# Products of zeros on TensorE ahead of the fold and behind the first image's last projection

## The chip, the cores and the metric

The kernel runs on one core of a Trainium2 chip. A core has a matrix engine (TensorE, PE in the profile, with its weight loads shown as PEld), a vector engine (VectorE, DVE), a scalar engine (ScalarE, ACT), a general engine (GpSimd, POOL), a queue engine (SyncE, SP), and 16 DMA engines. Each engine works through its own instructions in order and waits on semaphores for the others. The metric is the device time of one execution in microseconds (us).

## The reference

Eight images of 256 channels and 64 x 64 pixels pass through two layers, each with a residual:

```python
x = x + _L0_conv_ref(_gn(x), w_qkv, w_kg, b_kg, alpha, beta, w_proj)
x = x + _L1_conv_ref(_gn(x), w_off, b_off, w)
```

`_gn` normalises over 32 groups of 8 channels. The first layer projects to queries, keys and values; four heads of 64 channels attend to the 3 x 3 neighbourhood of each pixel:

```python
logits = jnp.einsum('bhdl,bhdkl->bhkl', q_flat, k_patch)
attn = jax.nn.softmax(logits, axis=2)
kernel = jnp.einsum('hkc,bhcl->bhkl', w_kg_g, cat) + b_kg.reshape(1, h, k2, 1)
out = alpha * conv_out + beta * attn_out
out = jnp.einsum('oc,bchw->bohw', w_proj, out)
```

Here `conv_out` and `attn_out` weight the 3 x 3 patches of the values by `kernel` and by `attn`. The second layer is a modulated deformable convolution: a 3 x 3 convolution gives 18 offsets and 9 masks for each pixel, four corners are gathered and blended at each of the nine positions, and a 256 x 256 product for each position sums them.

## The kernel before

Everything is fp32. On TensorE an fp32 product of 512 columns shows as two passes in the profile (two MATMUL records and two LDWEIGHTS records); a transpose shows as one. Channels lie on 128 partitions in two halves (`ct`), an image is cut into eight chunks of 8 rows (512 pixels).

The program is one stream per engine, written out by hand (`manual_schedule`): generators yield steps, and the main loop interleaves them. First `folded()` (line 225) multiplies `w_kgT` with `w_qkv` into `eff`, sixteen small products of nine columns, so that the generated kernel weights come straight from the normalised image. `first_stats` (L299) takes the statistics of image 0 on DVE while its chunks land, and `Norm` turns them into means and scales: `bn_aggr` (L192) into `mv`, a product with `gmat` (L197, `gn`), a few DVE steps on two columns, a second product (L208, `gv`), a square root on ACT and a reciprocal.

`attention(0)` then runs alone, without the second layer beside it, chunk by chunk. A chunk's work on TensorE, in the order of the profile: queries `psq` (L320, four passes for each half), keys `psk` (L351), logits `qk` (`products(0)`, L394), the generated weights `gen` (L437), `products(1)`, transposes `gt` (L456), and, between these, parts of the chunk before: `av` (L586), values `psv` (L351), `proj` (L602). It ends with `weights` (L529, transposes), `spread_weights` (L542) and `keys(0)` (L568, transposes). `masked` (L407, DVE) reads the logits of `products`, two tiles for each half of a chunk. `spread_weights` takes four PSUM tiles `wk`, one for each head, in a row; each head's product has nine rows of its own group of partitions, and DVE multiplies each tile by `near` (L550) into SBUF.

PSUM is shared out by pools: `ps_a` (four buffers of 512 columns, by far the most used), `ps_t` (two) and `ps_o` (two). A tile taken from a pool gets the buffer that was freed first, and its first writer waits for the last reader of the tile that had it before. In image 0, `proj` and `vk` use `ps_o` and `ps_t`; `eff`, `gn`, `gv`, `psq`, `psk`, `psv`, `qk`, `gen`, `gt`, `av`, `w` and `wk` all use `ps_a`, through `psum_a` (L182).

At the end of `attention(0)` the last `project` (L602), `add` (L613), `second_stats` (L617) and `Norm` follow each other, then `gn.means()` and `gn.ready()` as at the start. `prepare(0)` goes on from there: ACT scales the image into `z` (L773), TensorE transposes it (`ptab`, L791) for the table in DRAM from which the second layer gathers, and computes the offsets `om` (L838). From about 277 us the main loop runs the second layer of one image beside the attention of the next.

Of the kernel before, what the change touches and what calls it, by code (L numbers as in the profile page):

```python
# [9 lines left out]
F32 = mybir.dt.float32  # L10
# [7 lines left out]
P = 128  # L18
# [38 lines left out]
def preact_kernel(ctx: ExitStack, tc: tile.TileContext, a: dict, out: bass.AP):  # L57
# [17 lines left out]
    nc = tc.nc  # L75
# [3 lines left out]
    const = ctx.enter_context(tc.tile_pool(name="const", bufs=1))  # L79
# [81 lines left out]
    for i in range(min(2, B)):  # L161
# [7 lines left out]
        for o in range(H * WP, ENTRIES, P):  # L169
            n = min(P, ENTRIES - o)  # L170
# [10 lines left out]

    def psum_a(name):  # L182
        return ps_a.tile([P, 512], F32, tag="a", name=name)

    class Norm:

# [30 lines left out]
    def folded():  # L217

        ps = psum_a("eff")[:, : NT * HEADS * KK].rearrange(
            "p (c h k) -> p c h k", c=NT, h=HEADS  # L220
        )
        for ct in range(NT):
            for h in range(HEADS):
                for i in range(2):
                    nc.tensor.matmul(
                        ps[:, ct, h, :],
                        w_qkv[h // 2][:, 2 * (h % 2) + i, ct * P : (ct + 1) * P],
                        w_kgT[:, 2 * h + i, :],
                        start=(i == 0),
                        stop=(i == 1),  # L230
                    )
        return ps
# [62 lines left out]
    def first_stats(b, c):  # L295
        if c == 0:
            stats0[b] = p2.tile([P, NT, NC, 6], F32, tag="stats0", name=f"stats0_{b}")
        for ct in range(NT):
            nc.vector.bn_stats(  # L299
                stats0[b][:, ct, c, :],  # L300
                second[c][:, ct] if b == 1 else image[:, ct, c * N : (c + 1) * N],
            )
        if c == NC - 1:
            norm0[b] = Norm(stats0[b], f"0_{b}")
# [322 lines left out]
    def attention(b):  # L627

        xt = image
        first = b == 0  # L630
        jobs, due[:] = due[:], []
        gn = norm0[b]
        if b != 1:
            gn.means()
        stats = p2.tile([P, NT, NC, 6], F32, tag="stats", name=f"stats1_{b}")
        yield None
        gn = gn.gn if b == 1 else gn.ready()
        yield None
        xn = normed(xt, gn, 0, 2)
        for job in jobs[:1]:  # L640
            job()
        yield None
        d = added = None
        for c in range(NC):
            if c != 1:
                a_ = Attention(b, c, xn, stats)
                a_.q(0)
                if added:
                    added.second_stats()
                if c in (2, 5, 6, 7):  # L650
                    yield None
                a_.q(1)
                yield None if c == 4 else "quiet"
            else:
                a_ = follows
            ahead_of = c + 1 < NC
            at = 2 * (c % 2)
            a_.k(0)
            if ahead_of:
                xn = normed(xt, gn, c + 1, at, cts=(0,))  # L660
            yield None if ahead_of else "quiet"
            a_.k(1)
            if ahead_of:
                normed(xt, gn, c + 1, at, cts=(1,))
            if first:
                for n in (c - 1, c)[: 1 + (c == NC - 1)]:
                    if n >= 0:
                        first_stats(1, n)
            yield None if ahead_of else "quiet"
            if d and not first:  # L670
                d.keys(0)
            a_.products(0)
            for job in jobs[c - 1 : c] * (c in (2, 3)):
                job()
            yield None if c in (2, 3) else "quiet"
            a_.generated()
            a_.masked(0)
            yield None
            a_.products(1)
            a_.turned()  # L680
            yield "quiet"
            if d:
                d.weighted(0)
            else:
                a_.v(0)
            a_.masked(1)
            a_.summed()
            yield None
            a_.logits_1()
            a_.carry_k()  # L690
            if d:
                d.keys(1)
                d.carry_v()
                yield None
                a_.v(0)
                a_.logits_2()
                a_.softmax_1()
                yield None
                d.weighted(1)
                a_.twisted()  # L700
            else:
                a_.v(1)
                a_.logits_2()
                yield None
                a_.softmax_1()
                a_.twisted()
                follows = Attention(b, 1, xn, stats)
                follows.q(0)
            yield None
            if d:  # L710
                a_.v(1)
            else:
                follows.q(1)
            a_.softmax_2()
            a_.softmax_3()
            yield None
            if d:
                d.add(0, d.project(0))
                yield None
            a_.weights()  # L720
            if first and c == NC - 1:
                norm0[1].means()
            if d:
                d.add(1, d.project(1))
                added = d
            yield None
            a_.spread_weights()
            if first and c == NC - 1:
                norm0[1].ready()
            if first:  # L730
                a_.keys(0)
            yield None
            d = a_
        if not first:
            d.keys(0)
        added.second_stats()
        yield None
        d.weighted(0)
        yield "quiet"
        d.keys(1)  # L740
        yield "quiet"
        d.weighted(1)
        yield "quiet"
        if not first:
            later[0]()
        yield "quiet"
        d.add(0, d.project(0))
        d.add(1, d.project(1))
        d.second_stats()
        gn = Norm(stats, f"1_{b}")  # L750
        yield None
        if not first:
            later[1]()
        yield "quiet"
        gn.means()
        yield None
        gn.ready()
        yield gn.gn
# [424 lines left out]
    def finished(b, c, m):  # L1183
        if m == 0:
            state["y"] = p1.tile([P, NT, N], F32, tag="y", name=f"y_{b}_{c}")
        nc.scalar.copy(state["y"][:, m], state["po"][m])
# [14 lines left out]
        mybir.EngineType.Pool,  # L1201
    }
    with tc.manual_schedule(engines=ordered):
        ps = folded()
        for c in range(NC):
            first_stats(0, c)
        fold(ps)
        steps = fronts()
        for n in range(STEPS):
            next(steps, None)  # L1210

        for n in range(4):
            next(steps, None)
        for i in range(6):
            gather(i)
        next(steps, None)
        scale(0)
        scale(1)
        next(steps, None)
        sum_corners(0)  # L1220
        for i in range(6, LEAD, 2):
            next(steps, None)
            if holds:
                nc.gpsimd.memset(holds.pop(), 0.0)
            if i == 8 or i == 12:
                sum_corners(i // 2 - 2)
            gather(i)
            gather(i + 1)
            if i in (6, 10, 14):
                scale(i // 2 - 1)  # L1230
                scale(i // 2)
        next(steps, None)
        done = STEPS + STEPS_AHEAD
        last = None
        for n in range(B * SLOTS + 1):
            late, last = last, None
            if n > 0 and n % KK == 0:
                last = divmod(n // KK - 1, NC)
            for m in range(NT):
                if n < B * SLOTS:  # L1240
                    if m == 0:
                        transposes(*divmod(n, SLOTS))
                    if not last:
                        ahead(NB * n + 2 * m)
                if late and m == 0:
                    stored(*late)
                if n > 0:
                    product(*divmod(n - 1, SLOTS), m)
                if last:

                    finished(*last, m)
                    ahead(NB * n + 2 * m)
                    if n == B * SLOTS:
                        stored(*last, slice(m, m + 1))

                h = NT * n + m + 1
                goal = h * STEPS
                while (done - STEPS - STEPS_AHEAD) * STEPS < goal:
                    state["quiet"] = next(steps, True)
                    done += 1  # L1260
                if n < B * SLOTS:
                    gathers(NB * n + 2 * m)
# [76 lines left out]
```

## Time and profile before

| what | us |
|---|---|
| median of 3 runs | 4612.72 (4606.46 to 4614.89) |
| the profiled execution's own time | 4635.28 |
| its span, first to last instruction | 4633.3 |
| TensorE busy in the span | 4480.2 |
| first TensorE product (fold) | 16.73 |
| last projection of image 0 ends its issue | 224.5 |

The profile is of one execution. In the timeline each row gives the start, the time from the first start to the last end, the engine, the line, the operation with its tiles (written <- read), its size, the number of instructions, and in brackets how long the engine was idle before it and what ended that. A row of waits gives the total in us, how often, and the longest. The granted clock of TensorE is 1.00 or 0.50 in this profile, and it changes in steps of 3.41 us.

### The profile page before, as it was taken

How to read it: one execution, taken by the hardware profiler on the slowest of the kernel's cores; microseconds unless marked ns; L12 is line 12 of the kernel's file. 1: busy time of each engine (PE TensorE's matmuls, PEld its weight loads, DVE VectorE, ACT ScalarE, POOL GpSimd, SP SyncE). 2: the span in 40 equal slices, each digit the busy share in tenths (PEclk: the TensorE clock that was granted, in tenths of full speed). 3: DMA queues.
4: the chain of work that ended last, by engine and by line, in shares of the span. 5: the costliest groups of instructions: out<-in, count | busy, mean ns of one | idle time of the engine just before them, and what ended most of it. 6: DMA issues, size and time to landing. Idle time of an engine off the chain costs nothing.

```text
span 4633.3 us, 77608 instructions
## 1 busy us (share of the span) xinstructions
PE 4480.2 (97%) x25344; PEld 2332.3 (50%) x25344; DVE 4130.8 (89%) x10183; ACT 2514.2 (54%) x5280; POOL 2783.1 (60%) x2850
## 2 busy tenths in 40 slices
PE   8989999999999999999999999999999999998888
PEld 4445554555545555455554555555554555543344
DVE  6669999999999999999989999999999999988777
ACT  3345556555565555555555555655556555554444
POOL 0046655666555665566655665556655666568887
PEclk9999999999999999999999999999999999999999
DMA  4078889888998899988899888998899888899998
GB/s 143 28 230 294 304 312 368 314 301 303 310 385 297 294 312 320 369 295 306 301 338 331 298 307 311 354 331 297 299 315 373 296 287 302 296 335 333 352 336 317
DMA packets 445761, 1412.46 MB, mean 305 GB/s; under 512 B 46430, under 2 KB 63070, under 8 KB 445228
## 3 DMA queue, kind: packets, MB, share of 16 engines
q0 software_dynamic: 331776, 1208.11, 74.4%
q1 hardware_dynamic: 111836, 196.82, 11.8%
q8 instruction: 199, 3.26, 0.3%
q10 hardware_dynamic: 1744, 2.59, 0.2%
q14 instruction: 206, 1.69, 0.1%
HBM read 1275.97 MB, written 131.36 MB: 304 GB/s over the span
## 4 chain that ended last, share of the span: by engine, by line
PE 86%; DVE 4%; DMA 4%; issue 2%; POOL 2%; ACT 1%; another core or an unknown queue 0%; POOLq 0%; DVEq 0%; ACTq 0%; SPq 0%
PE po L1171 38%; PE pt L1146 10%; PE psk L351 5%; PE psq L320 5%; PE proj L602 5%; PE psv L351 5%; PE om L838 5%; PE av L586 3%; DVE s L1116 3%; PE vk L568 2%; PE qk L394 2%; DMA g<-table,idx 2%; PE wk L542 2%; PE gen L437 1%; DMA x<-in_x_dram 1%
## 5 line engine op out<-in xcount | busy, mean ns | idle before, releaser
L1092 POOL DMA_INDIRECT g<-table,idx x2304 | 2670.7, 1159 | 1352.4 <-DVE s L1116 409.1
L1116 DVE SCALAR_TENSOR_TENSOR s<-g,wt,s 128x256 f32<-128x256 f32 x6912 | 2822.9, 479 | 185.8 <-ACT s L1108 127.2
L1171 PE MATMUL po<-vt,w_conv 128*128 128x512 f32 x4608 | 2198.1, 602 | 0.4 <-issue 0.3
L1171 PEld LDWEIGHTS po<-vt,w_conv 128*128 128x128 f32 x4608 | 813.9, 192 | 774.8 <-issue 765.4
L1108 ACT ACTIVATE s<-g,wt 128x256 f32<-128x256 f32 x2304 | 1053.5, 511 | 204.8 <-DMA g<-table,idx 133.1
L1149 ACT COPY vt<-pt 128x512 f32<-128x512 f32 x1152 | 618.2, 589 | 456.5 <-PE pt L1146 330.8
L1146 PE MATMUL pt<-ident,s 128*128 128x128 f32 x4608 | 646.1, 280 | 76.4 <-ACT vt L1149 32.5
L1146 PEld LDWEIGHTS pt<-ident,s 128*128 128x128 f32 x4608 | 527.2, 142 | 340.9 <-issue 197.8
L838 PE MATMUL om<-xn,w_off 128*32 128x512 f32 (+1 forms) x2560 | 272.4, 553 | 0.0
L351 PE MATMUL psv<-xn,w_qkvT 128*128 128x512 f32 (+1 forms) x576 | 251.5, 564 | 3.7 <-issue 2.8
L351 PE MATMUL psk<-xn,w_qkvT 128*128 128x512 f32 (+1 forms) x576 | 246.8, 557 | 0.0
L320 PE MATMUL psq<-xn,w_qkvT 128*128 128x512 f32 x512 | 240.6, 600 | 2.8 <-issue 2.5
L602 PE MATMUL proj<-acc,w_projT 128*128 128x512 f32 x512 | 239.6, 593 | 0.7 <-ACT acc L593 0.7
L328 ACT COPY q<-psq 128x512 f32<-128x512 f32 x128 | 74.8, 586 | 234.5 <-PE psq L320 228.4
L407 DVE TENSOR_TENSOR qk<-qk,near_k 128x400 f32<-128x400 f32 x256 | 134.8, 569 | 73.7 <-PE qk L394 36.8
L593 ACT COPY acc<-av 128x512 f32<-128x512 f32 x128 | 74.8, 584 | 227.9 <-PE pt L1146 164.0
L362 ACT COPY k<-psk 128x512 f32<-128x512 f32 (+1 forms) x144 | 79.1, 551 | 202.3 <-PE psk L351 179.7
L586 PEld LDWEIGHTS av<-wk,vk 100*64 100x64 f32 x4096 | 133.0, 137 | 107.2 <-issue 64.1
L838 PEld LDWEIGHTS om<-xn,w_off 128*32 128x32 f32 x2560 | 75.0, 109 | 207.7 <-issue 201.3
L573 ACT COPY vk<-vk 100x512 f32<-100x512 f32 x256 | 138.3, 592 | 62.2 <-PE vk L568 52.8
L550 DVE TENSOR_TENSOR wk<-wk,near 100x512 f32<-100x512 f32 x256 | 158.7, 682 | 12.9 <-PE wk L542 12.8
L586 PE MATMUL av<-wk,vk 100*64 100x64 f32 x4096 | 154.4, 225 | 12.1 <-issue 11.4
(107 smaller groups left out, 3387.6 us busy)
## 6 DMA issues: line engine op xcount, KB each, us to landing
table<-ts SPq DMA_DIRECT2D x128, 384.0 KB
g<-table,idx POOLq DMA_INDIRECT x2304
x<-x SPq DMA_DIRECT2D x56, 512.0 KB
r<-x SPq DMA_DIRECT2D x56, 512.0 KB
out_dram<-r SPq DMA_DIRECT2D x56, 512.0 KB
x<-in_x_dram SPq DMA_DIRECT2D x52, 512.0 KB
table<-ts SPq DMA_DIRECT2D x128, 128.0 KB
second<-in_x_dram SPq DMA_DIRECT2D x8, 512.0 KB
```

Of the source, the lines that this page charges most:

```text
L320: nc.tensor.matmul(ps, w_qkvT[:, ct, m * P : (m + 1) * P], window(self.xn, ct, 4), start=(ct == 0), stop=(ct == NT - 1),)
L351: nc.tensor.matmul(ps[:, : (hi - lo) * W], w_qkvT[:, ct, o : o + P], self.xn[:, ct, lo:hi, 1 : W + 1], start=(ct == 0), stop=(ct == NT - 1),)
L550: nc.vector.tensor_mul(wk.rearrange("p (t n) -> p t n", n=T * T), ps[:NK].rearrange("p (t n) -> p t n", n=T * T), near.unsqueeze(1).to_bro ...
L586: nc.tensor.matmul(av[64 * h : 64 * h + 64, g, t * T * T : (t + 1) * T * T], self.vk[:, t, o : o + 64], self.wk[2 * g + h][:, i * n + t * ...
L602: nc.tensor.matmul(ps, w_projT[:, ct, m * P : (m + 1) * P], self.acc[:, ct].rearrange("p (t y x) -> p y t x", y=T, x=T), start=(ct == 0), ...
L838: nc.tensor.matmul(self.ps[32 * g : 32 * g + 32, cols], w_off[:, ct, k, :], window(self.xn, ct, k)[:, ys], start=(n < 4), stop=(tail >= 0),)
L1092: nc.gpsimd.indirect_dma_start(out=g, out_offset=None, in_=tables[b % 2], in_offset=bass.IndirectOffsetOnAxis(ap=found[b, c][0][:, j, k : ...
L1108: nc.scalar.activation(s, g[:, 0:C], AF.Copy, scale=w[:, 0:1])
L1116: nc.vector.scalar_tensor_tensor(s, g[:, q * C : (q + 1) * C], w[:, q : q + 1], s, ALU.mult, ALU.add)
L1146: nc.tensor.transpose(pt[ct][:, j, :], s[:, ct * P : (ct + 1) * P], ident)
L1149: nc.scalar.copy(v[:, ct, :], pt[ct].rearrange("p b n -> p (b n)"))
L1171: nc.tensor.matmul(po[m], w_conv[:, ct, k, m * P : (m + 1) * P], v[:, ct, :], start=(k == 0 and ct == 0), stop=(b + 1 < B and k == KK - 1 ...
```

## The change

A tile `warm` of 128 x 512 zeros is set by DVE; a PSUM tile `warming` is taken from `ps_a`; and `kept_warm(n)` multiplies the zeros by themselves into it n times. It is called with nine before `folded()`, and with two, for the first image alone, behind the last projection. Nobody reads `warming`. `psum_a`, which takes the tile, is shown above the new lines.

```diff
     def psum_a(name):
         return ps_a.tile([P, 512], F32, tag="a", name=name)
+
+    warm = const.tile([P, 512], F32, name="warm")
+    nc.vector.memset(warm, 0.0)
+    warming = psum_a("warm")
+
+    def kept_warm(n, size=512):
+        for i in range(n):
+            nc.tensor.matmul(
+                warming[:, :size], warm[:, :P], warm[:, :size], start=True, stop=True
+            )
 
     class Norm:
...
         d.add(1, d.project(1))
         d.second_stats()
         gn = Norm(stats, f"1_{b}")
+        if first:
+            kept_warm(2)
         yield None
...
     with tc.manual_schedule(engines=ordered):
+        kept_warm(9)
         ps = folded()
         for c in range(NC):
             first_stats(0, c)
```

## The prediction

> **What bounds the kernel now.** I read the page's busy table and chain first, then the waits of TensorE in the first image, then the timeline around the two places of the change, then the granted clock in short windows.
>
> ```profile
> span 4633.3 us, 77608 instructions
> ...
> PE 4480.2 (97%) x25344; PEld 2332.3 (50%) x25344; DVE 4130.8 (89%) x10183; ACT 2514.2 (54%) x5280; POOL 2783.1 (60%) x2850
> ...
> PE 86%; DVE 4%; DMA 4%; issue 2%; POOL 2%; ACT 1%; another core or an unknown queue 0%; POOLq 0%; DVEq 0%; ACTq 0%; SPq 0%
> ```
>
> TensorE (PE) is the bound: 97% busy and 86% of the chain that ended last. What delays it is not made up elsewhere. That holds for the first image's attention above all: between 55 and 215 us, seven of its eight chunks, TensorE's waits are these two groups, 2.0 us in 160.
>
> ```profile
> PE qk L394 <- ACT k L362: 1.2, 7, 0.2
> PE gv L208 <- DVE wk L550: 0.8, 1, 0.8
> ```
>
> The start of the span, from the timeline (start, duration, engine, line, tiles, instructions):
>
> ```profile
> 16.73 7.00 PE L225 MATMUL eff<-w_kgT,w_qkv 96*128 96x9 f32 x32 [16.73 <-DMA w_kgT<-in_w_kgT_dram]
> 21.81 0.58 DVE L192 BATCH_NORM_AGGREGATE mv<-stats 128x2 f32<-128x48 f32 x2
> 23.57 0.57 PE L197 MATMUL gn<-mv,gmat 128*128 128x2 f32 x2
> 26.86 5.40 PE L320 MATMUL psq<-xn,w_qkvT 128*128 128x512 f32 x8 [1.26 <-issue]
> 28.70 0.34 PEld L320 LDWEIGHTS psq<-xn,w_qkvT 128*128 128x128 f32 x1 [0.52 <-issue]
> 31.23 0.19 PEld L320 LDWEIGHTS psq<-xn,w_qkvT 128*128 128x128 f32 x1 [0.24 <-issue]
> ```
>
> TensorE is empty until the fold at 16.73 us. The first query passes follow at 0.85 us (26.86 to 30.37) and then at 0.43, and a weight load falls from 0.34 to 0.19: half clock until 30.3 us, although the clock column reads 1.00 there (its first record is at 30.3). Windows of 3.41 us, the step in which clock records change (us, PE busy, PEld, DVE, ACT, POOL, clock, DMA):
>
> ```profile
> 224.88:228.30 3.41, 0.52 (x4) 0.44 (x4) 2.64 (x9) 0.00 (x0) 0.00 (x0) 1.00 0.42 156
> 228.30:231.71 3.41, 1.58 (x7) 1.21 (x8) 2.66 (x9) 2.60 (x5) 0.75 (x1) 0.50 0.00 0
> 231.71:235.12 3.41, 3.41 (x17) 2.50 (x19) 1.02 (x2) 3.41 (x7) 1.33 (x2) 0.50 0.15 32
> 235.12:238.54 3.41, 3.41 (x40) 0.95 (x32) 0.00 (x0) 1.99 (x4) 0.00 (x0) 1.00 0.97 222
> ```
>
> A thin window is followed by half clock, a full one by full clock. Counting in each window the time in which columns stream (0.43 us for a pass of 512, 0.107 for 128, and for the fold's 9 columns next to nothing), every window at full clock that streams under 0.36 of its length is followed by half clock, none over 0.44 is; from half clock every window over 0.84 leads out and none under 0.76 does. The fold streams 0.07 of its windows, though the busy column shows it at 100%.
>
> **What the change adds.** One memset on DVE, 0.52 us by the row of line 133 (two in 1.03), at 2.2 us, where DVE idles until 6.09: nothing. Nine fp32 products, 18 passes, ahead of the fold; two, four passes, behind the last projection. No transfer and no instruction moves on ACT, POOL or SP. And one thing that the diff does not say: the tile `warming` is taken from pool ps_a, which has four buffers, and is last written by the two late products. Until then it holds its buffer. In the built program, every ps_a tile of the first image's attention rotates through three buffers, so each waits for the reader of the tile three back rather than four.
>
> **1. Nine products: 0.3 us won.** They start at about 2.7 us. A clock released after one or two windows gives an end between 2.7 + 2.7 + 15 x 0.43 = 11.8 and 2.7 + 6.8 + 10 x 0.43 = 13.8 us; both are before 16.73, so they lie in idle time (never released, 18 x 0.85 ends at 18.0 and puts the fold 1.3 us late). Then nothing streams for over 13 us until 26.86. By the windows, the clock falls two to five us after the last product, so the queries start at half clock as before: the 1.7 us of 26.86 to 30.3 (four passes at 0.85 in place of 0.43) stay. Only if the fall comes after 16.73 does part of the fold, 0.213 us per pass, run faster. That is worth at most 1.1 us, since `gn` at 23.57 can go back to 22.45, the end of `mv`. Ends -1.1 and +1.3; I take -0.3, as most phases of the window give nothing.
>
> **2. Two products: nothing.**
>
> ```profile
> 226.30 0.59 DVE L192 BATCH_NORM_AGGREGATE mv<-stats 128x2 f32<-128x48 f32 x2
> 226.94 0.38 PE L197 MATMUL gn<-mv,gmat 128*128 128x2 f32 x2 [2.48 <-DVE mv L192]
> 230.95 3.46 PE L791 MATMUL ptab<-ident,z 128*128 128x128 f32 x15 [0.23 <-ACT z L773]
> ```
>
> The last projection pass is issued until 224.46; four passes of 0.43 end at 226.2, 0.75 us before `gn` can start, so DVE's chain covers them (at half clock, 227.9, they cost 1.0). After them 4.7 us without streaming remain until 230.95, against 6.5: wherever the windows fall, one of them stays under 0.36. The transposes run at half clock again. If the clock stayed full, 15 transposes would need 1.6 us in place of 3.2, partly held by ACT's z (0.74 each), and the first offsets 0.35 less: 1.4 us. Ends -1.4 and +1.0; taken 0.
>
> [...] By the share per window the step is 0.
>
> **3. Three buffers: 17 us lost.** One steady chunk:
>
> ```profile
> 95.20 1.12 PE L542 MATMUL wk<-wsb,spread 9*100 9x512 f32 x8
> 96.25 1.08 PE L568 MATMUL vk<-ident,v 128*100 128x128 f32 x8
> 97.16 3.63 PE L320 MATMUL psq<-xn,w_qkvT 128*128 128x512 f32 x8
> ...
> 96.33 2.48 DVE L550 TENSOR_TENSOR wk<-wk,near 100x512 f32<-100x512 f32 x4 [0.34 <-PE wk L542]
> ```
>
> The four spread products of `spread_weights` run side by side, in four buffers, and free TensorE after 1.05 us. With three, the fourth must wait until DVE has multiplied the first: 96.33 + 0.68 + 0.05 (a TensorE start after DVE's end, shortest seen) = 97.07. Alone it then needs two passes, 0.86 us (1.05 by the group's row) before the transposes `vk` can follow: 97.93 to 98.12 in place of 96.25, 1.68 to 1.87 us. Everything behind it on TensorE's queue, `vk`, then the next chunk's queries and keys, is late by that, and DVE and ACT wait for them.
>
> Two smaller waits. In `products(1)` the second tile of logits needs the buffer of the second tile of `products(0)`:
>
> ```profile
> 82.13 1.06 DVE L407 TENSOR_TENSOR qk<-qk,near_k 128x400 f32<-128x400 f32 x2 [3.29 <-PE qk L394]
> 83.01 0.93 PE L394 MATMUL qk<-k,q 64*64 64x100 f32 x32
> ```
>
> DVE ends at 83.19, so 83.24 in place of 83.02: 0.2 us. And `av` at 84.52 then needs what DVE frees about 84.6: 0.1. All other tiles of a chunk find their buffer free, since the readers end 0.2 us or more ahead. A chunk loses 1.75 + 0.2 + 0.1 = 2.05 (1.9 to 2.2).
>
> Chunk 0 has `v` in place of `av`: 0.2 + 0.3, and its spread stall falls into the half clock of 50.80 to 54.22, 1.6 to 2.5 us: together 2.5 (2.1 to 3.0). Sum: 7 x 2.05 + 2.5 = 16.9, ends 15.4 and 18.4. No cover is left: TensorE is all but continuous from 55 to 215 us, and nothing later waits for a fixed time.
>
> **Sum.** -0.3 + 0 + 16.9 = 16.6 us. The profiled execution took 4635.28 us (span 4633.3), 22.6 over the median of the runs, 4612.72; I put the difference on the median: 4629.3. A measurement tells about 0.2%, 9 us, from no change; this is 0.36%.
>
> **Rivals.** (a) The waits bite as in 3: +16.6, 4629. For it: the waits in the built program, and a queue without slack. (b) The clock wins and the buffers cost little, the other side: the clock stays full over both gaps, -1.7 -1.1 at the start and -1.4 at 228, -4.2, 4608.5; not slower. It decides only if the fourth spread product's stall is under 0.5 us, which needs DVE done with the first before 95.7; its input ends at 96.30. (c) The stall turns into half clock: a window of 3.41 us with 1.8 us of stall streams about 0.6, over 0.43; but if nine-row products count for little, it falls to about 0.4, and up to eight chunks lose another 1.7 us each: +16.6 + 13.6, 4643. (d) The products do not do what the words say: zeros release no clock, and the fold starts 1.3 us late: 4631, inside (a).
>
> **Chances.** (a) with (d) 0.80, (c) 0.08, (b) and whatever else hides the stall 0.12, of which 0.03 is faster by more than 0.2%. Range: (a) is 15.4 - 1.1 - 1.4 to 18.4 + 1.3 + 1.0, so 4626 to 4633; half-clock windows of 1.7 us that fall otherwise in the last image and the spread of the runs (4606 to 4615) add 6 to 7 on each side: 4619 to 4639. Slower 0.88, same 0.09, faster 0.03.
>
> **What the new profile would show.** Per chunk of the first image, about 1.9 us of TensorE idle inside line 542's group, released by DVE at the line of `wk`; a chunk of 25.5 us in place of 23.4; the last projection of that image 17 us later. Full clock by 10 us, half again before 27, half also in the windows behind the two products. I am wrong if the fourth spread product starts beside the other three, or if the queries of chunk 0 start at 0.43 us a pass.

## The result and the profile after

The changed kernel takes 4638.74 us (median of 4 runs, 4632.60 to 4645.20) where the old one takes 4609.59 (4605.16 to 4614.89): ratio 1.0065, interval 1.0052 to 1.0078. It is slower by 29 us. The forecast was slower by 16.6 us, 4629.3, with a range of 4619 to 4639. On the old median now measured, 16.6 us give 4626, and the range becomes 4616 to 4636: the sign was right, the size was too small by over two fifths, and the time lies above the range. The result is what rival (c) gave, +30.2.

The two profiled spans cannot be set against each other: the old kernel's profiled execution took 26 us more than the median of its runs. Laid side by side, the TensorE products of the new profile start 29.3 us later at 219 us of the old span, and still 25.5 us later at 2451; behind that the old execution loses this lead in single steps, 17 us of it in its last 490 us. So what follows reads the first image, where the kernels differ, by its stages.

The page of the new profile, busy time and chain:

```profile
span 4630.6 us, 77649 instructions
...
PE 4505.7 (97%) x25366; PEld 2333.2 (50%) x25366; DVE 4134.4 (89%) x10184; ACT 2522.6 (54%) x5280; POOL 2781.2 (60%) x2850
...
PE 86%; DMA 4%; DVE 4%; POOL 4%; issue 2%; ACT 1%; POOLq 0%; another core or an unknown queue 0%; ACTq 0%; DVEq 0%; SPq 0%
```

TensorE is the bound as before, and its busy sum has grown by 25.5 us, of which the 22 added passes account for only 12.15 us by their two timeline rows (10.27 and 1.88, shown below). Time was also lost inside instructions, not between them. TensorE's waits between 55 and 245 us, again seven chunks (us in total, times, longest):

```profile
PE wk L552 <- DVE wk L560: 5.4, 7, 0.8
PE qk L404 <- ACT k L372: 1.2, 7, 0.2
```

The predicted wait is there, once a chunk, released by VectorE's multiply of `wk`. The chunk shows what it costs; TensorE first, then DVE (start, duration, engine, line, tiles, instructions):

```profile
75.47 1.11 PE L552 MATMUL wk<-wsb,spread 9*100 9x512 f32 x6
77.35 1.10 PE L552 MATMUL wk<-wsb,spread 9*100 9x512 f32 x2 [0.77 <-DVE wk L560]
78.38 1.36 PE L578 MATMUL vk<-ident,v 128*100 128x128 f32 x8
79.53 5.06 PE L330 MATMUL psq<-xn,w_qkvT 128*128 128x512 f32 x8
...
76.61 2.57 DVE L560 TENSOR_TENSOR wk<-wk,near 100x512 f32<-100x512 f32 x4 [0.34 <-PE wk L552]
```

Three spread products run side by side, the fourth stands 0.77 us and then runs alone for 1.1, so that `vk` starts 2.91 us after the group did; before, 1.05. That is 1.86 us. But then the queries take 5.06 us in place of 3.63. The windows of 3.41 us on the clock's own boundaries (us, PE busy, PEld, DVE, ACT, POOL, clock, DMA) show why:

```profile
72.19:75.61 3.42, 3.42 (x14) 1.48 (x15) 1.41 (x5) 0.94 (x3) 0.00 (x0) 1.00 0.00 0
75.61:79.02 3.41, 2.64 (x14) 1.01 (x15) 3.08 (x5) 0.00 (x0) 0.00 (x0) 1.00 0.41 154
79.02:82.43 3.41, 3.41 (x9) 1.86 (x7) 3.41 (x7) 1.17 (x2) 0.00 (x0) 0.50 0.41 118
82.43:85.85 3.42, 3.42 (x9) 1.45 (x9) 0.18 (x1) 1.17 (x2) 0.00 (x0) 1.00 0.09 35
```

The window with the stall, though TensorE is busy for 2.64 of its 3.41 us, is followed by one at half clock. The clock records of the trace show half clock from 51.7, 79.0, 106.3, 133.7, 161.0, 188.3, 215.6 and 242.9 us, once in each of the eight chunks, where the old profile has it in the first alone. A chunk takes 27.25 us (from one spread group to the next, 75.47 to 102.72) where it took 23.41 (71.79 to 95.20).

The start and the late place, from the timeline:

```profile
2.74 10.27 PE L191 MATMUL warm<-warm 128*128 128x512 f32 x18 [2.74 <-DVE warm L186]
15.94 5.52 PE L235 MATMUL eff<-w_kgT,w_qkv 96*128 96x9 f32 x32 [2.94 <-DMA w_kgT<-in_w_kgT_dram]
25.15 6.70 PE L330 MATMUL psq<-xn,w_qkvT 128*128 128x512 f32 x8 [1.42 <-DVE xn L279]
...
254.20 1.88 PE L191 MATMUL warm<-warm 128*128 128x512 f32 x4
256.84 0.38 PE L207 MATMUL gn<-mv,gmat 128*128 128x2 f32 x2 [0.76 <-DVE mv L202]
260.11 0.47 PE L803 MATMUL ptab<-ident,z 128*128 128x128 f32 x1 [1.60 <-ACT z L785]
260.81 3.08 PE L803 MATMUL ptab<-ident,z 128*128 128x128 f32 x15 [0.23 <-ACT z L785]
```

The nine end at 13.0 us. The first record of the clock is of 1.00, at 7.4, and from 17.6 it is 0.50, 1.7 us into the fold, which takes 5.5 in place of 7.0; the queries start 1.7 us earlier (0.8 of it because the fold's weights landed earlier) and run at half clock, all eight passes. The two late products end 0.76 us before `gn` can start, and nearly all of the transposes run at half clock still (259.9 to 263.4).

### The profile page after: what moved, and what is told of

It reads as the page before. It is cut to its first block, busy times and chain, and to the rows that moved or that the text cites. A ratio compares the mean times of both kernels' runs of the same rounds, so it can differ in the third digit from the quotient of the medians.

```text
span 4630.6 us, 77649 instructions
## 1 busy us (share of the span) xinstructions
PE 4505.7 (97%) x25366; PEld 2333.2 (50%) x25366; DVE 4134.4 (89%) x10184; ACT 2522.6 (54%) x5280; POOL 2781.2 (60%) x2850
## 4 chain that ended last, share of the span: by engine, by line
PE 86%; DMA 4%; DVE 4%; POOL 4%; issue 2%; ACT 1%; POOLq 0%; another core or an unknown queue 0%; ACTq 0%; DVEq 0%; SPq 0%
PE po L1183 37%; PE pt L1158 10%; PE psq L330 5%; PE psv L361 5%; PE psk L361 5%; PE proj L612 5%; PE om L850 5%; PE av L596 3%; POOL g L1104 3%; DMA g<-table,idx 3%; DVE s L1128 3%; PE vk L578 3%; PE qk L404 2%; PE wk L552 2%; PE gen L447 1%
## 5 line engine op out<-in xcount | busy, mean ns | idle before, releaser
L330 PE MATMUL psq<-xn,w_qkvT 128*128 128x512 f32 x512 | 251.1, 623 | 3.3 <-DVE xn L279 1.7
```

Of the source, the lines that this page charges most:

```text
L330: nc.tensor.matmul(ps, w_qkvT[:, ct, m * P : (m + 1) * P], window(self.xn, ct, 4), start=(ct == 0), stop=(ct == NT - 1),)
```

## The experiments

The theories. A: the held buffer makes the fourth spread product wait, and the thin window that this leaves halves the clock. B: the products of zeros upset the clock for long after, and the buffer matters little. C: the wait alone costs the whole 3.8 us of a chunk. Later, R against T: whether a product counts for the clock by the share of the array's rows that it uses, or by its time alone. Times are medians against the old kernel measured beside them, which took 20 to 24 us less there than above (4585.55 to 4589.28), so only times that stand side by side are compared; a stage is read from the profile.

**A buffer of its own for each call.**

```diff
-    warming = psum_a("warm")
     def kept_warm(n, size=512):
+        warming = psum_a("warm")
```

> Both groups of products stay, nine and two, but each call takes a PSUM tile of its own, so the buffer goes back to the pool after the call and the first image's attention has four buffers again. Theory A (the held buffer makes the fourth spread product wait, and the thin window that this leaves halves the clock): a chunk of the first image takes 23.4 us again, no half clock between 60 and 215 us, the whole 0 to 3 us faster than before. Theory B (the products themselves upset the clock for long after, the buffer matters little): chunks of 27 us, still about 29 us slower.

Measured: 4585.79 us against 4587.94, ratio 0.9998 (0.9989 to 1.0007). Chunks take 23.42 us, as in the old kernel to 0.01, and between 31 and 228 us the only half clock is one window at 51.3, as the old kernel has one at 50.8. Its waits of TensorE between 55 and 215 us:

```profile
PE qk L403 <- ACT k L371: 1.2, 7, 0.2
PE gv L217 <- DVE wk L559: 0.8, 1, 0.8
```

These are the two rows of before; the row of `wk` is gone. With the same 22 passes of zeros, and four buffers, the 29 us are gone. B falls.

**The buffer held, nothing warmed.**

```diff
-        kept_warm(9)
+        kept_warm(1, 2)
...
-            kept_warm(2)
+            kept_warm(1, 2)
```

> The buffer is held as in the change, but nothing is warmed: one product of two columns ahead of the fold and one of two columns behind the last projection, in place of nine and two full ones. Theory A: chunks of 27.2 us with one window of half clock each, 29 to 31 us slower than before, since the 1.7 us won at the start are gone as well. Theory B: chunks of 23.4 to 25.5 us, at most 17 us slower.

Measured: 4617.89 us against 4587.94, ratio 1.0062 (1.0047 to 1.0078), 30 us slower, with chunks of 27.24 us and half clock in each. Two products of two columns are enough, if the tile lives from the one to the other. The loss is the buffer's.

**One more product in the stall.**

```diff
             for h in range(HEADS):
+                if self.b == 0 and h == HEADS - 1:
+                    kept_warm(1)
                 ps = psum_a(f"wk_{self.u}_{h}")
```

> The change, and in the first image one more product of zeros (two passes, 0.86 us) ahead of each fourth spread product, inside the 0.8 us in which TensorE waits for VectorE. It takes the place of the idle time, not of the wait. Theory A in two parts (wait 2.1 us a chunk, half clock 1.7 us a chunk): the window fills, the clock stays at 1.00, chunks of 25.5 to 25.8 us, 16 to 19 us slower than before. Theory C (the wait alone costs 3.8 us a chunk and the half clock lies beside it): chunks of 27.2 us or more, 29 us slower or more.

Measured: 4607.09 us against 4587.94, ratio 1.0039 (1.0023 to 1.0054): 19 us slower where the change itself cost 29, by adding work. Chunks take 25.78 us, and no window between 30 and 240 us is at half clock. A chunk, and the windows around a later fourth product:

```profile
71.93 1.11 PE L554 MATMUL wk<-wsb,spread 9*100 9x512 f32 x6
72.97 1.12 PE L191 MATMUL warm<-warm 128*128 128x512 f32 x2
74.03 1.10 PE L554 MATMUL wk<-wsb,spread 9*100 9x512 f32 x2
75.06 1.08 PE L580 MATMUL vk<-ident,v 128*100 128x128 f32 x8
75.97 3.61 PE L330 MATMUL psq<-xn,w_qkvT 128*128 128x512 f32 x8
```

```profile
97.39:100.80 3.41, 3.41 (x11) 0.80 (x10) 2.58 (x4) 0.00 (x0) 0.00 (x0) 1.00 0.31 120
100.80:104.21 3.41, 3.41 (x15) 2.05 (x15) 3.27 (x6) 1.61 (x3) 0.00 (x0) 1.00 0.12 39
```

`vk` starts 3.13 us after the group, later than in the changed kernel, and yet the queries end earlier, since they are back at 3.61 us. So the chunk's 3.83 us are two costs. Here 2.36 are left without half clock, a little of it the added product's own, and 1.47 are gone; the 32-row kernel below separates them without added work. C falls.

**The nine alone.**

```diff
-        if first:
-            kept_warm(2)
```

> The nine products alone; without a later use the buffer goes back to the pool after them. Theory A: chunks of 23.4 us, 0 to 3 us faster than before, the same as with both groups in tiles of their own, because the two late products win nothing. If the two late products do hold the clock, this kernel ends the transposes behind the first image's attention about 1.4 us later than the one with both groups. Theory B: chunks of 27 us, 29 us slower.

Measured: 4588.61 us against 4587.94, ratio 0.9999 (0.9990 to 1.0008), chunks of 23.42 us: without a later use the buffer goes back. From the last projection pass to the first offsets it takes 10.37 us, with both groups in tiles of their own 10.43, in the old kernel 10.47. The two late products win nothing.

**Nine rows, and 64 rows, in place of 128.** Theory A needed one thing more: I had counted the stall's window at about 0.6 of its length, by the time in which columns stream, and that is over the 0.44 above which the old profile shows no halving. Both kernels have tiles of their own, and differ from the first experiment in the nine products alone (here for 9 rows; the other has 64):

```diff
-    def kept_warm(n, size=512):
+    def kept_warm(n, size=512, rows=P):
...
-                warming[:, :size], warm[:, :P], warm[:, :size], start=True, stop=True
+                warming[:, :size], warm[:rows, :P], warm[:rows, :size], start=True, stop=True
...
-        kept_warm(9)
+        kept_warm(9, rows=9)
```

> Products in tiles of their own, four buffers; but the nine ahead of the fold use 9 rows of the array in place of 128 (the first 9 partitions of both operands), with the same 512 columns and the same 18 passes. Theory R (a product counts for the clock by the share of the rows that it uses): 9 of 128 rows is 0.07 of the window, the clock is never released, 18 passes at 0.85 us from 2.7 us end at about 18.1, the fold starts 1.3 us later than without, and the first clock record stands near 30 us. Theory T (any streaming counts by its time): full clock by 7 to 10 us, as with 128 rows.

> The same with 64 of 128 rows. Theory R: 0.50 of the window, under the 0.76 that never led out of half clock: not released either, the products end at about 18.1 us. Theory T, or a count in which half the rows are enough: full clock by 7 to 10 us.

The rows of the products in the two timelines, 9 rows first, then 64:

```profile
2.73 15.73 PE L190 MATMUL warm<-warm 9*128 9x512 f32 x18 [2.73 <-DVE warm L186]
18.39 7.00 PE L234 MATMUL eff<-w_kgT,w_qkv 96*128 96x9 f32 x32
```

```profile
2.74 15.72 PE L190 MATMUL warm<-warm 64*128 64x512 f32 x18 [2.74 <-DVE warm L186]
18.39 6.99 PE L234 MATMUL eff<-w_kgT,w_qkv 96*128 96x9 f32 x32
```

Neither brought full clock: 18 passes took 15.7 us, 0.87 each, against 10.06 with 128 rows; the eight query passes from 28.68 us still took 5.48 and 5.08 us, where eight take 3.61 at full clock, and the first records at full clock stand at 32.3 and 31.5 us. The fold starts 1.6 us later than in the first experiment. As many passes, as many columns, at least as long, fewer rows: this goes against T. R is borne out as far as that fewer rows did not bring full clock; that it goes by the share of the rows, these two do not show. (One time each, 4586.52 and 4594.65 against 4585.55, which tells nothing of a few us.)

**The change, with spread products of 32 rows.**

```diff
-                    spread[32 * h : 32 * h + KK],
-                    self.wsb[32 * h : 32 * h + KK],
+                    spread[32 * h : 32 * h + 32],
+                    self.wsb[32 * h : 32 * h + 32],
```

> The change with its held buffer, and the spread products with 32 rows each in place of 9 (the rows added hold zeros, so the products are the same). Nothing else moves, and the wait for VectorE stays. Theory R: the thin window of a chunk goes from about 0.24 to 0.40 of its length, between the 0.36 that always halved the clock and the 0.44 that never did: half clock in fewer of the chunks or in none, chunks of 25.3 to 25.8 us where it is gone. Theory T: rows do not matter, all chunks stay at 27.2 us.

Measured: chunks of 25.57 us, no half clock between 57 and 230 us, 4598.11 us against 4585.55 in one run each. The wait stays; here are the chunk and its window, with the one behind it:

```profile
73.22 1.11 PE L552 MATMUL wk<-wsb,spread 32*100 32x512 f32 x6
75.10 1.10 PE L552 MATMUL wk<-wsb,spread 32*100 32x512 f32 x2 [0.77 <-DVE wk L560]
76.13 1.08 PE L578 MATMUL vk<-ident,v 128*100 128x128 f32 x8
77.05 3.61 PE L330 MATMUL psq<-xn,w_qkvT 128*128 128x512 f32 x8
```

```profile
73.28:76.70 3.42, 2.65 (x14) 1.02 (x14) 3.04 (x5) 0.00 (x0) 0.00 (x0) 1.00 0.40 153
76.70:80.11 3.41, 3.41 (x13) 1.71 (x12) 3.41 (x7) 1.66 (x3) 0.00 (x0) 1.00 0.40 117
```

This is the window of the changed kernel once more, 2.65 us busy in place of 2.64, 14 passes, the same idle 0.77; only the rows of the eight spread passes differ (the added ones hold zeros, in the weights and in the moving operand), and the clock stays at 1.00. A chunk with the wait and without the half clock takes 25.57 us; so the waits and the lone product cost 2.15 us and the half clock 1.68.

**The fourth product behind the next transposes.**

```diff
-            a_.spread_weights()
+            a_.spread_weights(range(3) if first else range(HEADS))
...
             if first:
                 a_.keys(0)
+                a_.spread_weights([3])
```

> The change with its held buffer, but in the first image the fourth spread product stands behind the eight transposes of keys(0), so that VectorE has freed its buffer by then. Theory A: the 0.8 us in which TensorE waits are filled with work of the kernel, the fourth product still costs its own 1.1 us, since it runs alone: chunks of 24.6 to 25.0 us without half clock, 9 to 13 us slower than before. If the wait were not for VectorE's multiply, the chunk would stay near 27 us.

Measured: 24.91 us in four of the five middle chunks, 26.60 in the one that meets a half-clock window (178.3), 4598.89 us against 4585.55 in one run each.

```profile
75.41 1.11 PE L553 MATMUL wk<-wsb,spread 9*100 9x512 f32 x6
76.45 1.08 PE L579 MATMUL vk<-ident,v 128*100 128x128 f32 x8
77.46 1.10 PE L553 MATMUL wk<-wsb,spread 9*100 9x512 f32 x2
```

The idle time is gone, and 1.1 us of the lone product stays: even with its order mended, a buffer less costs a product that no longer runs beside others (two passes take 1.10 us here, eight side by side 1.12 in the old kernel). The 13 us are at the upper end of what was expected; the one chunk at half clock was not expected.

**Products in all gaps.** The one version that could beat both kernels keeps the four buffers and fills every gap at both places.

```diff
-        kept_warm(9)
+        kept_warm(16)
         ps = folded()
+        kept_warm(2)
...
             nc.tensor.matmul(ps[:, 0:NT], gmat, mv[:, :, 0], start=True, stop=True)
+            if name in ("0_0", "1_0"):
+                kept_warm(1, 320)
...
             nc.tensor.matmul(ps[:, 0:NT], gmat, self.d, start=True, stop=True)
+            if name in ("0_0", "1_0"):
+                kept_warm(1)
+                kept_warm(1, 256)
```

> Products in tiles of their own, four buffers, and products of zeros in all the gaps of both places: sixteen ahead of the fold and two behind it, one of 320 columns between the two small products of the group norm, one and a half behind them; the same around the norm behind the last projection (two, then 320 columns, then one and a half). Theory A: no window streams under 0.44, so the first queries run at 0.43 us a pass and the transposes behind the first image's attention at full clock; the first offsets start 2 to 4 us earlier than the 234.3 us of before, the whole 2 to 4 us faster, 0.05 to 0.1%, at the edge of what five rounds tell. Against it: a product that stands in the way of the norm's small products puts them up to 0.9 us late at each of four places, which takes the gain back.

Measured: 4586.28 us against 4589.28, ratio 0.9993 (0.9984 to 1.0002): no difference that can be told. Its timeline at the late place:

```profile
225.79 1.88 PE L190 MATMUL warm<-warm 128*128 128x512 f32 x4
228.68 0.78 PE L190 MATMUL warm<-warm 128*128 128x320 f32 x2
229.97 1.54 PE L190 MATMUL warm<-warm 128*128 128x512 f32 x4
231.70 0.33 PE L807 MATMUL ptab<-ident,z 128*128 128x128 f32 x1 [0.20 <-ACT z L789]
234.73 4.07 PE L854 MATMUL om<-xn,w_off 128*32 128x512 f32 x40
```

There the clock did stay at full (eight of the transposes take 1.09 us, where in the changed kernel fifteen took 3.08): from the last projection pass to the first offsets 9.36 us in place of 10.47. At the start the products stood in the way: the fold began at 19.17 and `gn` at 27.14 where the old kernel has 23.57, and the full clock of the first queries (3.68 us for their eight passes in place of 5.40) won back only half of that (first keys at 33.80 against 32.09). Behind the last projection warming won 1.1 us in this run; it is not to be seen in the whole.

## Why the prediction was right or wrong

**Nine products** (taken -0.3, ends -1.1 and +1.3): right. They lie in idle time, and the clock falls before the queries in every kernel that has them. What they gave went with when it fell: at 16.3 and 17.2 us next to nothing (queries at 26.91 and 26.80, in the old kernel at 26.86), at 17.8, 18.7 and 18.9 about 1 us (25.72, 25.83 and 25.97). The changed kernel's own 25.15 has 0.8 us of an earlier landing in it. The kernels with 9 and 64 rows show what the other end would have been: the fold 1.6 us late.

**Two products** (taken 0): right, with no delay of `gn` and no gain, 10.43 against 10.37 us without them. In the changed kernel itself it is 10.05, since there the clock is full again from 263.4. Short gaps did not keep the clock up: in the old kernel TensorE's idle times there are 2.48, 0.84 and 1.60 us, and the clock is at half from 228.3; in the changed kernel they are 0.76, 0.93 and 1.60, and it is at half from 259.9. It stayed full in the kernel with products in all three gaps.

**Three buffers** (taken +16.9): the mechanism was right, its own size too. The prediction had 2.05 us a chunk from the waits; the kernel with 32-row spread products, which has the waits alone, shows 25.57 - 23.42 = 2.15, and its last projection pass of the first image starts 16.4 us behind that of the kernel with tiles of its own (240.36 against 223.92). One sign was misread: the text looked for about 1.9 us of idle TensorE in the group, and the idle time is 0.77; the rest of the 1.86 us is the fourth product running alone, as the text's own sum had it.

**The step that failed** is rival (c), or rather the sentence that made it one: that a window with the stall "streams about 0.6, over 0.43". I counted a pass by its time, whatever its rows. By time the 0.6 was right: 0.64, my count from the changed kernel's records, and yet half clock follows. But the spread products use 9 of 128 rows each. With 32 rows in the same 2.65 us of busy time, and with 9 rows and an added product of 128 in the stall, the clock stayed at 1.00. The half clock behind it costs 1.68 us a chunk, some 13 us over the image (the last projection pass starts at 253.77 in place of 240.36), which is what is missing between 16.6 and 29. The text named the possibility ("if nine-row products count for little") and its price, 13.6 us, and gave it 0.08. It had the means to do better: the same text had counted that the fold, whose nine columns stream next to nothing, leaves the clock at half (0.07 of its windows, busy at 100%, half clock until 30.3 us), so that "busy" was known not to be enough; for rows no such row was sought. The range stopped at 4639, under that rival's 4643, though its mechanism touches all eight chunks at once and so does not shade into the likeliest case but jumps.

**Where the loss passes on:** as predicted, nothing takes it back. The last projection pass of the first image starts at 253.77 us in place of 223.87, 29.9 later, and the whole is 29.2 slower. The kernel that only holds the buffer shows the same against the one with tiles of its own: 29.5 us at that pass (253.46 and 223.92), 32.1 in the whole.

## What to carry to other kernels

A tile that is taken once and written twice, far apart, holds its buffer all the way between; in a pool of four that is a quarter of it, and the cost shows at whatever takes four in a row (here the spread products, 2.15 us a chunk). An added wait on the bounding engine should be priced twice, by itself and by what the clock does behind it: here 2.15 and 1.68 us a chunk. Before products are added to keep the clock up, look at their rows and at every gap: here nine products of 128 rows were followed by full clock at 7.4 us, nine of 64 or of 9 were not while they ran, to 18.5, and behind the last projection two products left the transposes at half clock, where products in all three gaps kept it at full.

## What the runs showed of the hardware

Two windows with all but the same TensorE time were followed by different clocks. In the changed kernel the one from 75.61 us, with spread products of 9 rows, has 2.64 us of busy time in 14 passes, and the clock behind it is 0.50; in the kernel with 32-row spread products the one from 73.28 us has 2.65 us in 14 passes, and the clock behind it is 1.00. The idle time is 0.77 us in both. Weights and moving operand got the added rows together, so which of the two made the difference was not separated. Ahead of the fold, eighteen passes of 512 columns from 2.74 us on were followed by full clock from 7.4 us with 128 rows (the changed kernel), and only from 31.5 and 32.3 us, behind the first queries' start, with 64 and 9. How much a row weighs, and from what amount on the clock changes, these runs do not show.

In the changed kernel the halving repeats in step. A chunk of 27.25 us is eight windows of 3.41 less 0.06, so that the stall fell at nearly the same place of its window in each chunk, and all eight were hit. Where chunks take 24.91 us, one of the five middle ones was hit.

Not all of the half clock lies where TensorE is the bound. Seven windows of it lie in the last image of the changed kernel, where the chain that ended last runs, from 4150 us on, for 54% of the time over the gathers (28% their issue on POOL, 25% their transfers) and only for about 13% over TensorE. From these shares I estimate that it costs little there; that was not tried.
